# A gated cross-attention block with routed experts: the last four of 39 routed tiles in a block entered only when the count of used tiles is above 35

## The chip, the core and the metric

The kernel runs on one core of a Trainium2 chip. The metric is the time on the device in microseconds (us). Runs of the same program are summed up by their median. Beside them stands one profiled execution, from which every duration of a single instruction comes.

The engines are TensorE (PE in the profile; PEld is its weight load, PEldq its sequencer), VectorE (DVE), ScalarE (ACT), GpSimd (POOL) and SyncE (SP, which here only starts DMA transfers). Each has an instruction stream of its own, and they wait for each other by semaphores.

## What is computed

The reference is a cross-attention layer and a mixture-of-experts layer, both with a gate, on x of 4 x 512 rows of 256 numbers, all in 32-bit floats. Cut to what matters here:

```python
x = x + tanh(g_xattn[0]) * xattn(layernorm(x), ctx)   # 16 heads, 1601 context rows
h = layernorm(x)                                      # 2048 rows of 256
probs = sigmoid(h @ Wr.T + rb)                        # 8 routed experts
scores, idx = top_k(probs, 2)                         # 2 experts for each row
out = expert(h, shared)
for e in range(8):
    out = out + cw[..., e:e+1] * expert(h, e)         # cw: the score where e was picked, else 0
x = x + tanh(g_ffn[0]) * out
# expert(h, e) = (silu(h @ Wg.T) * (h @ Wu.T)) @ Wd.T, inner width 512
```

Each row has two picked experts, so there are 4096 pairs of row and expert. How they fall on the eight experts depends on the data.

## The kernel before, in words

The first three quarters of the time are the attention, with a written-out order of bursts; the change does not touch it. Then come the experts.

*Routing (find_places, invert, addresses).* The kernel computes only the picked pairs. It sorts the pairs by expert into tiles of 128 rows, and an expert's last tile may be partly empty. DVE counts the pairs per expert, derives how many tiles each expert uses (`used`, line 868) and sums these up along the experts (`end`, line 871), so that the last element of `end` is the number of used tiles. `tile_e` (line 912) holds the expert of each tile. Two small matrices, `token` and `dest`, hold for each tile the 128 source rows and the 128 result rows; where a tile has no pair, the address is out of bounds and the transfer of that row is dropped.

*The tiles.* The program is fixed before the data are known, so it has a tile for the worst case: `TILES = (TOP * NT + NR * (P - 1)) // P` is (2 * 2048 + 8 * 127) // 128 = 39 (line 110). The loop at line 1051 is unrolled over these 39. For tile i it has

- `own(i)` (line 1033): PE loads the tile's expert from `tile_e` into a register, which then selects the weights in `w_all`, where all eight experts lie;
- `half(i, gp, 0)` and `half(i, up, 2)` (line 993): the gate and the up product into PSUM, ahead of the second of them `turn(i - 1)`;
- the silu on ACT (line 1060) and the product `hid2[i]` on DVE (line 1062);
- `take(i + 1)` (line 984): PE turns the next tile's gathered rows, ACT copies them out of PSUM;
- `fetch(i + 3)` (line 973): POOL starts the gather of rows three tiles ahead, from `rows_x` into one of four buffers;
- `give(i - 1)` (line 1010): the down product of the tile before, a copy by DVE (line 1021), and the scatter by POOL into `rows_y` in HBM (line 1022). The scatters are declared free of each other.

`turn(i)` (line 1003) transposes `hid2[i]` on PE in four pieces, and ACT copies the result.

*Shared expert (fill).* The shared expert of all rows is cut into pieces; `fill(n)` places the next n of them where it stands. After the row of tiles two pieces stand, then `turn` of the last tile, one piece, and its `give`; then comes `fill(2 * NI)`, eight pieces (line 1100).

*The end.* Eight DMAs (line 1080) load `rows_y` into parts of `w_all` whose weights are used up; they wait for all scatters. `combine` (line 1085) adds the two weighted results to each row on DVE (line 1090) and starts the output DMAs (line 1095), among them four more pieces of the shared expert.

*Order.* From line 1037 on, a manual schedule keeps PE and POOL in the order of the text; the streams of ACT, DVE and SP are ordered by the framework's scheduler inside that part.

Of the kernel before, what the change touches and what calls it, by code (L numbers as in the profile page):

```python
# [8 lines left out]
FP = mybir.dt.float32  # L9
AF = mybir.ActivationFunctionType  # L10
# [15 lines left out]
def kernel(  # L26
# [782 lines left out]
    picks = [moe.tile(shp, FP, name=f"pick{k}") for k in range(TOP)]  # L809
    cws = [moe.tile([P, NTT], FP, name=f"cw{k}") for k in range(TOP)]  # L810
    tile_e = moe.tile([1, TILES], I32, name="tile_e")
    place = moe.tile([P, NJ], FP, name="place")
    at_tile = moe.tile([P, NJ], FP, name="at_tile")
    at_row = moe.tile([P, NJ], FP, name="at_row")
# [24 lines left out]
    def find_places():  # L839

        flat = both.rearrange("p t e -> p (t e)")
        before = ps_ms.tile([P, S], FP, tag="ms", name="before")[:, : NTT * NR]
        nc.tensor.matmul(before, lhsT=triu, rhs=flat, start=True, stop=True)
        total = ps_av.tile([P, S], FP, tag="av", name="total")[:, : NTT * NR]
        nc.tensor.matmul(total, lhsT=ones, rhs=flat, start=True, stop=True)
        tot = moe.tile(shp, FP, name="tot")
        nc.vector.tensor_copy(tot.rearrange("p t e -> p (t e)"), total)
        acc = [moe.tile(shp, FP, name=f"acc{k}") for k in range(2)]
        src, d, k = tot, 1, 0
        while d < NTT:  # L850
            dst = acc[k]
            nc.vector.tensor_copy(dst[:, :d, :], src[:, :d, :])
            nc.vector.tensor_tensor(
                dst[:, d:, :], src[:, d:, :], src[:, : NTT - d, :], ALU.add
            )
            src, d, k = dst, 2 * d, 1 - k
        count = src[:, NTT - 1, :]
        wide = [P, NR, NTT]
        full = moe.tile(wide, FP, name="full")
        marks = moe.tile([P, NTT], FP, name="marks")  # L860
        nc.vector.tensor_scalar(marks, steps[:, :NTT], float(P), None, ALU.mult)
        nc.vector.tensor_tensor(
            full,
            count.unsqueeze(2).to_broadcast(wide),
            marks.unsqueeze(1).to_broadcast(wide),
            ALU.is_gt,
        )
        used = moe.tile([P, NR], FP, name="used")
        nc.vector.tensor_reduce(used, full, AX.X, ALU.add)
        ends = [moe.tile([P, NR], FP, name=f"ends{k}") for k in range(2)]  # L870
        end, d, k = used, 1, 0
        while d < NR:
            dst = ends[k]
            nc.vector.tensor_copy(dst[:, :d], end[:, :d])
            nc.vector.tensor_tensor(dst[:, d:], end[:, d:], end[:, : NR - d], ALU.add)
            end, d, k = dst, 2 * d, 1 - k
        base = moe.tile([P, NR], FP, name="base")
        nc.vector.tensor_tensor(base, end, used, ALU.subtract)
        nc.vector.tensor_scalar(base, base, float(P), None, ALU.mult)
        row = moe.tile(shp, FP, name="row")  # L880
        nc.vector.tensor_tensor(row, src, tot, ALU.subtract)
        nc.vector.tensor_tensor(
            row, row, before.rearrange("p (t e) -> p t e", e=NR), ALU.add
        )
        nc.vector.tensor_tensor(
            row, row, base.unsqueeze(1).to_broadcast(shp), ALU.add
        )
        for k in range(TOP):
            nc.vector.tensor_tensor(hits, picks[k], row, ALU.mult)
            nc.vector.tensor_reduce(  # L890
                place[:, k * NTT : (k + 1) * NTT], hits, AX.X, ALU.add
            )

        nc.vector.tensor_scalar(
            at_tile, place, 1.0 / P, -(P - 1) / (2.0 * P), ALU.mult, ALU.add
        )
        nc.vector.tensor_scalar(at_tile, at_tile, 1.5 * 2.0**23, None, ALU.add)
        nc.vector.tensor_scalar(at_tile, at_tile, -1.5 * 2.0**23, None, ALU.add)
        nc.vector.scalar_tensor_tensor(
            at_row, at_tile, -float(P), place, ALU.mult, ALU.add  # L900
        )
        owner = [1, TILES, NR]
        past = moe.tile(owner, FP, name="past")
        nc.vector.tensor_tensor(
            past,
            end[0:1].unsqueeze(1).to_broadcast(owner),
            steps[0:1, :TILES].unsqueeze(2).to_broadcast(owner),
            ALU.is_le,
        )
        te = moe.tile([1, TILES], FP, name="te")  # L910
        nc.vector.tensor_reduce(te, past, AX.X, ALU.add)
        nc.vector.tensor_scalar(tile_e, te, float(NR - 1), None, ALU.min)


    PART = 8
# [68 lines left out]
    def take(i):  # L984
        ps = ps_ms.tile([P, S], FP, tag="ms", name="tx")[:, :H].rearrange(
            "p (c n) -> p c n", n=P
        )
        for c in range(2):
            nc.tensor.transpose(ps[:, c, :], xg[i % 4][:, c * P : (c + 1) * P], ident)  # L989
        xT[i] = work.tile([P, 2, P], FP, tag="xT", name=f"xT_{i}")  # L990
        nc.scalar.copy(xT[i], ps)  # L991

    def half(i, ps, off):
        for c in range(2):
            nc.tensor.matmul(  # L995
                ps,
                lhsT=xT[i][:, c, :],
                rhs=w_flat[:, bass.ds(owners[i] + (off + c) * I, I)],
                start=(c == 0),
                stop=(c == 1),  # L1000
            )

    def turn(i):
        ps = ps_av.tile([P, S], FP, tag="av", name="th").rearrange("p (f n) -> p f n", n=P)
        for f in range(NI):
            nc.tensor.transpose(ps[:, f, :], hid2[i][:, f * P : (f + 1) * P], ident)  # L1006
        hT2[i] = work.tile([P, NI, P], FP, tag="hT2", name=f"hT2_{i}")
        nc.scalar.copy(hT2[i], ps)
# [24 lines left out]
    def own(i):  # L1033
        e = nc.tensor.value_load(tile_e[0:1, i : i + 1], min_val=0, max_val=NR - 1)
        owners[i] = nc.tensor.snap(e * (6 * I))

    with tc.manual_schedule(engines={mybir.EngineType.PE, mybir.EngineType.Pool}):
        choose()
        fill(5)
        find_places()  # L1040
        fill(6)
        for part in range(NJ // PART):
            invert(part)
            fill(1)
        addresses()
        for i in range(3):
            fetch(i)
        weights()
        fill(3)
        take(0)  # L1050
        for i in range(TILES):
            own(i)
            gp = ps_g.tile([P, I], FP, tag="g", name="gp")
            half(i, gp, 0)
            if i:
                turn(i - 1)
            up = ps_u.tile([P, I], FP, tag="u", name="up")
            half(i, up, 2)
            sg = work.tile([P, I], FP, tag="sg")
            nc.scalar.activation(sg, gp, AF.Silu)  # L1060
            hid2[i] = work.tile([P, I], FP, tag="hid2", name=f"hid2_{i}")
            nc.vector.tensor_tensor(hid2[i], sg, up, ALU.mult)  # L1062
            if i + 1 < TILES:
                take(i + 1)
            fetch(i + 3)
            if i:
                give(i - 1)
        fill(2)
        turn(TILES - 1)
        fill(1)  # L1070
        give(TILES - 1)

        yk = {}
        for b in range(B):
            for k in range(TOP):
                yk[b, k] = w_all[:, TOP * b + k, 0:2, :].rearrange(
                    "p c (k h) -> p (c k) h", h=H
                )
                r = k * NT + b * S
                nc.sync.dma_start(  # L1080
                    out=yk[b, k],
                    in_=rows_y[r : r + S, :].rearrange("(t p) h -> p t h", p=P),
                )

        def combine(b):
            for t in range(NTB):
                for k in range(TOP):
                    xt = xs[b][:, t, :]
                    cw = cws[k][:, b * NTB + t : b * NTB + t + 1]
                    nc.vector.scalar_tensor_tensor(  # L1090
                        xt, yk[b, k][:, t, :], cw, xt, ALU.mult, ALU.add
                    )
                if t % 2:
                    r = b * S + (t - 1) * P
                    nc.sync.dma_start(
                        out=out[r : r + 2 * P, :].rearrange("(t p) h -> p t h", p=P),
                        in_=xs[b][:, t - 1 : t + 1, :],
                    )

        fill(2 * NI)  # L1100
        for b in range(2):
            combine(b)
        fill(NTB)
        for b in range(2, B):
            combine(b)
# [76 lines left out]
```

## Time and profile before

| | us |
|---|---|
| median of 3 runs | 1268.55 |
| lowest and highest | 1266.56 and 1268.7 |
| the profiled execution | 1266.34 |
| its span, first to last instruction | 1264.5 |
| first gate product of the tiles (PE, line 995) | 1004.64 |
| last gate product of the tiles starts | 1224.44 |
| last scatter (POOL, line 1022) | 1238.29 |
| first reload of results (SP, line 1080) | 1240.40 |

The span is the time between the first and the last instruction of one execution; the time of a run has about two microseconds more around it. In lines of a group, `x39` is the number of instructions, and a name like L1022 is the line of the source. In a line of the timeline the first number is the start, the second the duration of the group, and the bracket the time that the engine idled before it with what ended this. In windows each engine has its busy time and, in brackets, the number of its instructions. `<-` separates what is written from what is read.

### The profile page before, as it was taken

What the parts mean: (1) busy time and instruction counts of PE and PEld (TensorE: products, weight loads), DVE (VectorE), ACT (ScalarE), POOL (GpSimd) and SP (SyncE); (2) the same over time, 40 slices, a digit from 0 to 9 for tenths busy, and PEclk for the clock granted to TensorE, in tenths of its full rate; (3) what the DMA queues carried; (4) which work ended last, traced back from release to release, by engine and by line L of the source; (5) the groups of instructions that cost most, each with busy time, mean ns of one, the idle gap of its engine ahead of it and who ended that gap; (6) DMA issues with size and microseconds to landing.
All of it is one profiled execution on the core that took longest, in us unless ns stands there. A gap on an engine that the chain in (4) does not pass through costs nothing.

```text
span 1264.5 us, 19650 instructions
## 1 busy us (share of the span) xinstructions
PE 1246.0 (99%) x7742; PEld 558.7 (44%) x7742; DVE 686.9 (54%) x1294; ACT 592.6 (47%) x1139; POOL 133.7 (11%) x213
## 2 busy tenths in 40 slices
PE   7999999999999999999999999999999999999998
PEld 3533334333343433344343333344256566666665
DVE  5977666666676665666656656676026411121125
ACT  2265555556545555564565556555822122222220
POOL 2000200000013000000400000020000133333320
PEclk9999999999999999999999999999999999999999
DMA  5312000002001000200010000000092011111106
GB/s 123 102 40 64 1 14 14 1 1 53 14 1 31 14 2 1 53 14 1 4 27 14 1 13 14 1 18 1 1 335 81 18 38 42 47 40 43 35 9 199
DMA packets 30992, 48.29 MB, mean 38 GB/s; under 512 B 5487, under 2 KB 21745, under 8 KB 30902
## 3 DMA queue, kind: packets, MB, share of 16 engines
q1 hardware_dynamic: 26628, 38.14, 11.5%
q0 software_dynamic: 3744, 8.40, 2.1%
q8 instruction: 62, 1.02, 0.3%
q10 hardware_dynamic: 530, 0.50, 0.2%
q14 instruction: 28, 0.23, 0.1%
HBM read 32.99 MB, written 9.31 MB: 33 GB/s over the span
## 4 chain that ended last, share of the span: by engine, by line
PE 95%; DVE 2%; DMA 1%; issue 1%; ACT 0%; SPq 0%; DVEq 0%; ACTq 0%
PE sc L420 32%; PE av L441 17%; PE gp L995 5%; PE y_ps L1013 5%; PE up L995 5%; PE mx L361 4%; PE ms L338 4%; PE ms L312 3%; PE ms L490 3%; PE ms L293 3%; PE ms L502 2%; PE up L720 2%; PE gp L720 1%; PE th L1006 1%; PE sc L361 1%; PE op L743 1%
## 5 line engine op out<-in xcount | busy, mean ns | idle before, releaser
L372 DVE TENSOR_REDUCE mxs<-mx 128x1 f32<-128x512 f32 x744 | 480.1, 686 | 251.0 <-PE mx L361 247.1
L429 ACT ACTIVATE es<-sc 128x512 f32<-128x512 f32 x804 | 437.6, 594 | 341.1 <-PE mx L361 291.5
L361 PE MATMUL mx<-ks,qT 32*128 32x512 f32 (+1 forms) x1984 | 480.7, 549 | 0.0
L420 PE MATMUL sc<-qA,ks 32*128 32x512 f32 x1608 | 467.6, 637 | 0.8 <-DVE qA L415 0.8
L420 PEld LDWEIGHTS sc<-qA,ks 32*128 32x128 f32 x1608 | 131.2, 179 | 221.8 <-issue 165.3
L441 PE MATMUL av<-es,vs 128*32 128x512 f32 (+2 forms) x1864 | 227.8, 559 | 0.1
L361 PEld LDWEIGHTS mx<-ks,qT 32*128 32x128 f32 x1984 | 164.7, 183 | 4.0 <-issue 1.9
L441 PEld LDWEIGHTS av<-es,vs 128*32 128x32 f32 (+1 forms) x1864 | 37.1, 108 | 166.1 <-issue 161.2
L1062 DVE TENSOR_TENSOR hid<-sg,up 128x512 f32<-128x512 f32 x39 | 26.8, 688 | 138.2 <-PE up L995 138.2
L243 POOL TENSOR_SCALAR var<-var 128x4 f32<-128x4 f32 x6 | 1.4, 237 | 782.9 <-DVE first L240 782.9
L1060 ACT ACTIVATE sg<-gp 128x512 f32<-128x512 f32 x39 | 23.3, 597 | 115.7 <-PE gp L995 115.7
L995 PE MATMUL gp<-w_all,xT 128*128 x156 | 73.5, 593 | 0.9 <-ACT xT L991 0.9
L1013 PE MATMUL y_ps<-w_all,hT 128*128 x312 | 73.8, 379 | 0.0
L995 PE MATMUL up<-w_all,xT 128*128 x156 | 73.4, 593 | 0.0
L1013 PEld LDWEIGHTS y_ps<-w_all,hT 128*128 128x128 f32 x312 | 56.4, 190 | 6.5 <-issue 0.5
L338 PE MATMUL ms<-wv_t,ctx_t 96*128 96x256 f32 (+1 forms) x208 | 58.7, 404 | 0.1
L1022 POOL DMA_INDIRECT rows_y<-y,dest x39 | 39.5, 1014 | 149.1 <-DVE y L1021 149.1
L338 PEld LDWEIGHTS ms<-wv_t,ctx_t 96*128 96x128 f32 (+1 forms) x208 | 34.5, 185 | 37.9 <-issue 27.3
L975 POOL DMA_INDIRECT xg<-rows_x,token x39 | 40.2, 1030 | 48.1 <-DVE token L959 36.5
L312 PE MATMUL ms<-ctx_t,wk_t 96*128 96x401 f32 (+3 forms) x112 | 45.1, 524 | 0.0
L1021 DVE COPY y<-y_ps 128x256 f32<-128x256 f32 x39 | 16.6, 425 | 46.2 <-PE y_ps L1013 46.2
L991 ACT COPY xT<-tx 128x256 f32<-128x256 f32 x39 | 14.6, 375 | 54.5 <-PE tx L989 54.5
(164 smaller groups left out, 963.5 us busy)
## 6 DMA issues: line engine op xcount, KB each, us to landing
ks<-kd SPq DMA_DIRECT2D x63, 100.1 KB, 3.2
w_all<-in_wgT SPq DMA_DIRECT2D x8, 512.0 KB, 11.0
w_all<-in_wuT SPq DMA_DIRECT2D x8, 512.0 KB, 10.1
w_all<-in_wdT SPq DMA_DIRECT2D x8, 512.0 KB, 11.0
w_all<-rows_y SPq DMA_DIRECT2D x8, 512.0 KB, 8.3
ctx_t<-in_ctxT SPq DMA_DIRECT2D x3, 1200.8 KB, 8.0
xb<-in_x SPq DMA_DIRECT2D x4, 512.0 KB, 6.2
rows_x<-xn SPq DMA_DIRECT2D x4, 512.0 KB, 3.3
```

Source lines behind the costliest of these rows:

```text
L312: nc.tensor.matmul(ps[:, :n], lhsT=wk_t[r, c, h2 * P : (h2 + 1) * P], rhs=ctx_t[r, c, o : o + n], start=(c == 0), stop=(c == 1),)
L338: nc.tensor.matmul(ps[:n, : NH * HD], lhsT=ctx_t[r, c, o : o + n], rhs=heads[r, c, :, :HD], start=(c == 0), stop=(c == 1),)
L361: nc.tensor.matmul(ps[:, n * REST : (n + 1) * REST] if last else ps, lhsT=qT[i][slot_of(j), qb * P : (qb + 1) * P], rhs=ks[i % 3][slot_of( ...
L372: nc.vector.tensor_reduce(mxs[i][:, qb, j, c : c + 1], ps, AX.X, ALU.max)
L420: nc.tensor.matmul(ps[:n, :], lhsT=ks[i % 3][r, o : o + n], rhs=qA[i][r, :], start=True, stop=True)
L429: nc.scalar.activation(es[(i * NKT + kt) % 2, j][:n], ps[:n], AF.Exp, scale=SCALE)
L441: nc.tensor.matmul(av[i][j * HS : (j + 1) * HS, cols], lhsT=v_of(b, kt)[:n, g * HPG + j, :], rhs=es[(i * NKT + kt) % 2, j][:n, cols], star ...
L720: nc.tensor.matmul(ps, lhsT=w_sh[:, off + c, f * P : (f + 1) * P], rhs=x2T[:, c, b * S : (b + 1) * S], start=(c == 0), stop=(c == 1),)
L975: nc.gpsimd.indirect_dma_start(out=xg[i % 4], out_offset=None, in_=rows_x, in_offset=bass.IndirectOffsetOnAxis(ap=token[:, i : i + 1], axi ...
L995: nc.tensor.matmul(ps, lhsT=xT[i][:, c, :], rhs=w_flat[:, bass.ds(owners[i] + (off + c) * I, I)], start=(c == 0), stop=(c == 1),)
L1013: nc.tensor.matmul(ps, lhsT=hT2[i][:, f, :], rhs=w_flat[:, bass.ds(owners[i] + 4 * I + f * H, H)], start=(f == 0), stop=(f == NI - 1),)
L1022: ins = nc.gpsimd.indirect_dma_start(out=rows_y, out_offset=bass.IndirectOffsetOnAxis(ap=dest[:, i : i + 1], axis=0), in_=y, in_offset=Non ...
```

## The change

The body of the loop becomes a function `run_tiles(first, end)`. It is called for tiles 0 to 34 where the loop stood; `SURE` is 4096 // 128 + 8 // 2 - 1 = 35. Tiles 35 to 38 are called again inside `tc.If(n_used[0] > SURE)`, with a `take` of tile 35 ahead of them and `turn` and `give` of tile 38 behind. The two fills, the `turn` and the `give` that followed tile 38 now follow tile 34, ahead of the block. The count is copied to an integer, `tiles_used`, in `find_places`, and each of the five engines loads it into a register at tile 33. What follows the row of tiles stands in a manual schedule of its own behind the block. `fetch(i + 3)` still runs for tiles 35 to 37 ahead of the block.

The diff:

```diff
--- before.py
+++ after.py
@@ -809,6 +809,7 @@
     picks = [moe.tile(shp, FP, name=f"pick{k}") for k in range(TOP)]
     cws = [moe.tile([P, NTT], FP, name=f"cw{k}") for k in range(TOP)]
     tile_e = moe.tile([1, TILES], I32, name="tile_e")
+    tiles_used = moe.tile([1, 1], I32, name="tiles_used")
     place = moe.tile([P, NJ], FP, name="place")
     at_tile = moe.tile([P, NJ], FP, name="at_tile")
     at_row = moe.tile([P, NJ], FP, name="at_row")
@@ -910,6 +911,7 @@
         te = moe.tile([1, TILES], FP, name="te")
         nc.vector.tensor_reduce(te, past, AX.X, ALU.add)
         nc.vector.tensor_scalar(tile_e, te, float(NR - 1), None, ALU.min)
+        nc.vector.tensor_copy(tiles_used, end[0:1, NR - 1 : NR])
 
 
     PART = 8
@@ -1033,6 +1035,30 @@
     def own(i):
         e = nc.tensor.value_load(tile_e[0:1, i : i + 1], min_val=0, max_val=NR - 1)
         owners[i] = nc.tensor.snap(e * (6 * I))
+
+    def run_tiles(first, end):
+        for i in range(first, end):
+            own(i)
+            gp = ps_g.tile([P, I], FP, tag="g", name="gp")
+            half(i, gp, 0)
+            if i > first:
+                turn(i - 1)
+            up = ps_u.tile([P, I], FP, tag="u", name="up")
+            half(i, up, 2)
+            sg = work.tile([P, I], FP, tag="sg")
+            nc.scalar.activation(sg, gp, AF.Silu)
+            hid2[i] = work.tile([P, I], FP, tag="hid2", name=f"hid2_{i}")
+            nc.vector.tensor_tensor(hid2[i], sg, up, ALU.mult)
+            if i + 1 < end:
+                take(i + 1)
+            fetch(i + 3)
+            if i > first:
+                give(i - 1)
+            if i == SURE - 2:
+                n_used.append(nc.values_load(tiles_used, min_val=0, max_val=TILES))
+
+    n_used = []
+    SURE = TOP * NT // P + NR // 2 - 1
 
     with tc.manual_schedule(engines={mybir.EngineType.PE, mybir.EngineType.Pool}):
         choose()
@@ -1048,27 +1074,18 @@
         weights()
         fill(3)
         take(0)
-        for i in range(TILES):
-            own(i)
-            gp = ps_g.tile([P, I], FP, tag="g", name="gp")
-            half(i, gp, 0)
-            if i:
-                turn(i - 1)
-            up = ps_u.tile([P, I], FP, tag="u", name="up")
-            half(i, up, 2)
-            sg = work.tile([P, I], FP, tag="sg")
-            nc.scalar.activation(sg, gp, AF.Silu)
-            hid2[i] = work.tile([P, I], FP, tag="hid2", name=f"hid2_{i}")
-            nc.vector.tensor_tensor(hid2[i], sg, up, ALU.mult)
-            if i + 1 < TILES:
-                take(i + 1)
-            fetch(i + 3)
-            if i:
-                give(i - 1)
+        run_tiles(0, SURE)
         fill(2)
-        turn(TILES - 1)
+        turn(SURE - 1)
         fill(1)
-        give(TILES - 1)
+        give(SURE - 1)
+    with tc.If(n_used[0] > SURE):
+        with tc.manual_schedule(engines={mybir.EngineType.PE, mybir.EngineType.Pool}):
+            take(SURE)
+            run_tiles(SURE, TILES)
+            turn(TILES - 1)
+            give(TILES - 1)
+    with tc.manual_schedule(engines={mybir.EngineType.PE, mybir.EngineType.Pool}):
 
         yk = {}
         for b in range(B):
```

## The prediction

> **What bounds the kernel now.** I read the page first: busy shares, the clock row and the chain that ended last.
>
> ```profile
> PE 1246.0 (99%) x7742; PEld 558.7 (44%) x7742; DVE 686.9 (54%) x1294; ACT 592.6 (47%) x1139; POOL 133.7 (11%) x213
> ...
> PEclk9999999999999999999999999999999999999999
> ...
> PE 95%; DVE 2%; DMA 1%; issue 1%; ACT 0%; SPq 0%; DVEq 0%; ACTq 0%
> ```
>
> TensorE (PE) is busy for 99% of the span, in no slice below nine tenths of its clock, and carries 95% of the chain. PE work that goes away is worth its whole duration, as long as nothing takes its place. The second view is the busy time in windows: two of the last tiles, cut at the starts of their gate products (gp of tiles 36, 37 and 38), and the tail from just before the last result ends.
>
> ```profile
> core 0: us, PE busy (x) PEld busy (x) DVE busy (x) ACT busy (x) POOL busy (x), PEclk, DMA share, GB/s
> 1212.80:1218.62 5.82, 5.82 (x23) 3.60 (x22) 1.11 (x2) 1.45 (x3) 1.02 (x1) 1.00 0.05 19
> 1218.62:1224.44 5.82, 5.82 (x23) 3.60 (x22) 1.11 (x2) 1.45 (x3) 1.00 (x1) 1.00 0.01 0
> 1237.39:1264.50 27.11, 21.07 (x65) 11.89 (x63) 17.60 (x41) 2.39 (x4) 0.98 (x1) 1.00 0.70 232
> ```
>
> A tile takes 5.82 us, all of it PE at full clock; DVE needs 1.11 us of that and ACT 1.45. In the last 27 us DVE (17.60 us) and the DMA (0.70) come up beside PE: there a shorter PE alone would not move the end.
>
> Third, the DMA view of 1219 to 1239.5 us, in which the results of tiles 35 to 38 are scattered:
>
> ```profile
> q0 software_dynamic: 144, 0.00, 0.5%
> ...
> rows_y<-y,dest POOLq DMA_INDIRECT x4, 2.1
> ```
>
> Four scatters move 0.00 MB. The scatter of tile 34 (POOL, at 1213.71 us) lies in the first window above: 19 GB/s over 5.82 us are 110 KB, about 105 rows of 1 KB; the next window has none. So tile 34 holds rows and tiles 35 to 38 hold none: the count that the chip will read is 35, and 35 > 35 is false. The reference's routing, worked through for these inputs, agrees: 523, 614, 883, 116, 674, 638, 543 and 105 pairs per expert fill 5+5+7+1+6+5+5+1 = 35 tiles of 128.
>
> Fourth, the timeline from the last result to the end:
>
> ```profile
> 1235.66 1.89 PE L1013 MATMUL y_ps<-w_all,hT 128*128 x8
> ...
> 1238.29 0.98 POOL L1022 DMA_INDIRECT rows_y<-y,dest  x1 [6.36 <-DVE y L1021]
> ...
> 1240.40 7.83 SPq L1080 DMA_DIRECT2D w_all<-rows_y  x8
> ...
> 1244.40 0.88 DVE L1090 SCALAR_TENSOR_TENSOR xb<-w_all,cw,xb 128x256 f32<-128x256 f32 x2 [2.62 <-DMA w_all<-rows_y]
> ...
> 1249.41 1.88 PE L720 MATMUL up<-x2T,w_sh 128*128 128x512 f32 x4
> ...
> 1252.87 0.69 DVE L738 TENSOR_TENSOR hT<-sg,up 128x512 f32<-128x512 f32 x1
> ```
>
> Two strands run to the end: last result, copy, scatter, reload by DMA, combine on DVE; and beside it eight pieces of the shared expert on PE. They meet on DVE, which hardly rests from 1244.40 to 1261.4. PE has some room: its last up ends at 1251.29 and DVE takes it up at 1252.87, 1.6 us later; at the second of four pieces the room is 0.8, with 0.45 us of DVE idling behind it, 1.2 in all. I use 1.4.
>
> **The change, part by part.** Removed is the PE work of four tiles. The order around them stays: the fills and the last turn and give surround tile 34 as they did tile 38. So four whole steady periods go, 4 x 5.82 = 23.28 us. Of 39 gathers one is skipped (fetch 38), of 39 scatters four; they are empty and lie beside PE, worth 0.
>
> The last scatter has rows now. Tile 38's landed 2.1 us after its issue, empty; tile 34's moves 105 KB. The nearest row is that of the gathers, which landed in 2.2 (an empty one) to 2.9 us (a full one). I take +0.3 us (0 to 0.8) on the reload strand. One more DVE copy of one element stands in find_places; the nearest row is tile_e's on line 912, 164 ns. PE works on fills there; 0 to 0.2, I take 0.1.
>
> Five register loads of tiles_used come at tile 33, one per engine. The load of tile_e on PE has the price, with register arithmetic of 151 ns in the row after it:
>
> ```profile
> L1034 PEldq TENSOR_LOAD <-tile_e x39: 296/301/496, 1003.2 to 1222.1; - x39
> ```
>
> Some 0.45 us each. The last begins at 1222.1 us, and the gp that it serves at 1224.44: PE's sequencer runs 2.3 us ahead of its array, so tile 33's two loads, 0.9 us, stay under that cover (without it they would cost 0.5). What they wait for was written at about 979 us. Behind DVE's load stand hid and the y copy, behind ACT's the silu, behind POOL's the scatter; by the timeline these three idle 3.5, 3.0 and 3.5 us in each tile, and SP only waits there. I take 0.
>
> The block itself can only be bounded, since no branch stands in the trace. Below: each engine compares its own register and jumps, PE's jump under the 2.3 us lead. That is 0, and not less, because no tail can start before its data. Above: every engine must have finished and the last scatter landed before any goes on. From the end of the last y_ps (1237.55) copy, scatter and landing take until 1240.40, 2.85 us; 0.3 for the rows; 0.4 for a meeting of the engines (the program's end, after the last output has landed, has two in under 1 us). PE idles 3.5 us; less its room of 1.4, 2.1 us on the path, and SP's 0.7 us lie within that. Between: engines finish their own instructions, but no DMA is waited for. PE then waits until POOL's scatter is issued (1239.27), 1.7 us, +0.3 to meet, less 1.4 of room: 0.6. I take this 0.6. An engine's semaphore count must come out the same whether or not the block ran, so something has to be settled at the jump, but the landing has a wait of its own at line 1080.
>
> Two rules of the Trainium skill speak against the change. "Runtime: NRT & Kernel Launch", Instruction fetch mechanics: instructions stream in sequential blocks, and a jump to a target outside the two at hand waits for a fetch. The page has 62 packets, 1.02 MB, on an instruction queue: 16.5 KB each, one per 250 of PE's 15,484 matmuls and weight loads. The block holds 4 x 44 = 176 of these, with register instructions some 210, under one packet; on the other engines under 20. By the row the target is at hand and costs 0; if the rule bites, my estimate is one to two small landings in a row, 2 to 4 us. I go by the row. "TensorE: Matmul & The Clock Gate", Part 1: after an idle window of about 3.4 us PE runs at half clock for about as long. The clock row shows no such case, PE not idling so long in this phase; at 2.0 us idle it adds nothing, but the upper bound's 3.5 us sit on the threshold, and half speed for 3.4 us costs 1.7.
>
> The sum, the two strands added because DVE takes up both: -23.28 + 0.3 + 0.1 + 0.6 = -22.3 us. The profiled execution took 1266.34 us (span 1264.5 and 1.8 around it): it would take 1244.0. The median of the runs shown, 1268.55, is 2.2 above it; from there, 1246.2. I state the latter; the range takes in the former.
>
> **The rivals.** First, the engines meet at the block with the DMA included, and the reload strand's wait becomes everybody's. For it: all engines must agree, and the scatters count on semaphores of their own. Against it: no data makes PE wait. 2.1 + 0.1, with slow clock 3.9, in place of 1.0: 1247.4 to 1249.1.
>
> Second, PE's jump waits for instructions: 2 to 4 us on top of its 2.0, with no room left to hide them, 1248.2 to 1250.2. For it is the rule, against it the packet's size. The others' jumps would hide in their idle time.
>
> Third, slower: the block is entered. It decides at 36 used tiles; the expert with 638 pairs would need three more. Then no tile is saved and the row of tiles is cut in two. Tile 35's transposes and ACT copy come before its gp with no give to cover them (0.6 us); at the block's end turn waits for hid (PE's up ends 1228.48, hid 1229.28: 0.8) and give for the copy of th (0.8): together 2.2, and at the block's start and end 0.6 to 3.8 each. +3.4 to +9.8: 1272 to 1278. The empty scatters speak against it.
>
> That the block is skipped and the time not given back would need DVE or DMA to bind in the tile phase; they are busy 1.11 of 5.82 us and 5%.
>
> **How the numbers follow.** The likeliest case has 0.62 (own range 1243.5 to 1247.5), the first rival 0.24, the second 0.08, the third 0.03; 0.03 is for another order of DVE and ACT in a part now scheduled by itself, which may eat any share of the gain. This measurement tells about 0.2%, 2.5 us, from no change. Faster 0.95, same 0.02, slower 0.03. The range runs from the full 23.3 us below the quickest run (1266.56), 1243, to the second rival's end and a little slow clock, 1251.
>
> **What would show it.** Right: 35 scatters, and 156 - 16 = 140 gp matmuls of the tiles; a last scatter 22 to 24 us earlier; a PE gap of about 2 us between the last y_ps and the next gp of the shared expert; from the last scatter to the end 26 to 28 us (26.2 before). Wrong: that gap above 3 us, ending when the scatter lands (first rival), a clock under 1 behind it, a jump after which PE waits for nothing shown (second), 39 scatters (third). Tiles of other than 5.82 us would mean that the cut has disturbed the row itself.

## The result and the profile after

The changed kernel takes 1248.03 us in the median of 4 runs (1247.88 to 1248.13). Beside them 4 runs of the kernel before had a median of 1267.61 (1266.56 to 1268.7). The ratio is 0.9845, with an interval of 0.9828 to 0.9862. The profiled executions took 1266.34 us before and 1248.13 after: 18.2 us less, where the prediction's sum had 22.3. The forecast of 1246.2 was 1.8 us low, and the time lies in the range, but outside the likeliest case's own range (1243.5 to 1247.5).

The counts and windows of the page came as predicted. First the busy shares, the clock and the chain that ended last, from the page of the changed kernel:

```profile
PE 1224.7 (98%) x7654; PEld 545.2 (44%) x7654; DVE 683.4 (55%) x1287; ACT 586.7 (47%) x1127; POOL 128.7 (10%) x208
...
PEclk9999999999999999999999999999999999999999
...
PE 1%; DMA 1%; DVE 0%; SPq 0%; issue 0%; DVEq 0%
...
L997 PE MATMUL gp<-w_all,xT 128*128 x140 | 66.0, 593 | 0.9 <-ACT xT L993 0.9
```

PE's busy time falls by 21.3 us and the gate products go from 156 to 140: four tiles are gone. The chain that ended last was followed back for only 2 or 3% of the span, to PE's first product behind the block; the profile has no releaser there and stops. It therefore tells about the tail alone, and that PE's 95% are missing from it is no finding.

The windows, one tile (from the gp of tile 33 to that of tile 34) and the tail from just before the last scatter, and the DMA view of 1193 to 1217 us:

```profile
1195.81:1201.63 5.82, 5.82 (x24) 3.60 (x22) 1.11 (x2) 1.45 (x3) 2.04 (x2) 1.00 0.08 25
1215.40:1246.30 30.90, 22.55 (x64) 12.68 (x62) 18.00 (x40) 2.39 (x4) 1.00 (x1) 0.91 0.63 207
```

```profile
q0 software_dynamic: 288, 0.30, 3.9%
...
rows_y<-y,dest POOLq DMA_INDIRECT x4, 2.4
```

A tile still takes 5.82 us, all PE. The packets of three scatters fall into the DMA view; those of the last one, of tile 34, are in the view of 1213 to 1219 us, and carry rows too:

```profile
q0 software_dynamic: 48, 0.11, 5.2%
```

The new thing is in the second window: the tail is longer, and PE's clock in it is 0.91, where it was 1.00.

The timeline from the last result to the end (PE, DVE, POOL and SP; some rows left out):

```profile
1212.85 1.89 PE L1015 MATMUL y_ps<-w_all,hT 128*128 x8
...
1215.04 1.95 PE L720 MATMUL gp<-x2T,w_sh 128*128 128x512 f32 x4 [0.30 <-PEq L1082]
1215.48 1.00 POOL L1024 DMA_INDIRECT rows_y<-y,dest  x1 [6.33 <-DVE y L1023]
1216.83 1.88 PE L720 MATMUL up<-x2T,w_sh 128*128 128x512 f32 x4
...
1217.97 7.93 SPq L1097 DMA_DIRECT2D w_all<-rows_y  x8
...
1221.97 0.48 DVE L1107 SCALAR_TENSOR_TENSOR xb<-w_all,cw,xb 128x256 f32<-128x256 f32 x1 [6.77 <-DMA w_all<-rows_y]
...
1222.37 0.68 DVE L738 TENSOR_TENSOR hT<-sg,up 128x512 f32<-128x512 f32 x1
...
1230.77 2.85 DVE L1107 SCALAR_TENSOR_TENSOR xb<-w_all,cw,xb 128x256 f32<-128x256 f32 x7
...
1233.54 0.68 DVE L738 TENSOR_TENSOR hT<-sg,up 128x512 f32<-128x512 f32 x1
...
1234.28 7.38 PE L743 MATMUL op<-w_sh,hT 128*128 128x256 f32 x26 [2.67 <-DVE hT L738]
```

And two lines of the kernel before that answer to the hT and op lines:

```profile
1241.10 0.69 DVE L738 TENSOR_TENSOR hT<-sg,up 128x512 f32<-128x512 f32 x1 [3.08 <-PE up L720]
...
1253.61 5.88 PE L743 MATMUL op<-w_sh,hT 128*128 128x256 f32 x26 [1.03 <-DVE hT L738]
```

Read it from the top. At the jump PE stands still for 0.30 us. The last scatter starts at 1215.48, 22.81 us earlier than before (1238.29). The reload follows 2.49 us later (2.11 before). Then DVE takes up a combine *first* and idles 6.77 us until the first reload has landed. The first hT (silu of the gate times up, a product of the shared expert that its down product `op` on PE needs) stands behind it at 1222.37, though its up product was done at 1218.71. Before, DVE made that hT at 1241.10, ahead of the first combine. Counted from the last scatter, the four hT start at 2.81, 6.90, 11.21 and 14.58 us before, and at 6.89, 10.75, 14.69 and 18.06 us after. The last is 3.48 us later. The whole timelines show what stands ahead of it on DVE: 23 combines after, 17 before. Seven combines take 2.85 us, 0.41 each, so my estimate for the six more is 2.5 us; 0.6 is the first hT, which DVE used to make while it waited for the reload; 0.38 is the later start of the reload. Together that is 3.5 us. From the last hT to the last instruction it is 11.62 us before and 12.74 after, 1.12 more. The gain in the profiles is therefore -22.81 + 3.48 + 1.12 = -18.2 us.

The 1.12 have to do with the 26 down products, which take 7.38 us in place of 5.88. The windows of the changed kernel show the clock behind it (after PE's busy time come PEld, DVE, ACT and POOL, then the granted clock, DMA share and GB/s):

```profile
1225.00:1230.00 5.00, 4.87 (x14) 2.24 (x12) 4.92 (x13) 0.60 (x1) 0.00 (x0) 1.00 1.05 343
1230.00:1235.00 5.00, 1.42 (x4) 0.94 (x5) 4.62 (x11) 0.00 (x0) 0.00 (x0) 0.89 1.09 367
1235.00:1240.00 5.00, 5.00 (x20) 4.19 (x19) 2.94 (x7) 0.00 (x0) 0.00 (x0) 0.77 0.26 92
```

Between 1230 and 1235 us PE waits for hT twice, 1.03 and 2.67 us, and in the next window it is busy throughout at a clock of 0.77. The windows of before are all at 1.00.

One thing has to be known for the comparisons below: executions of every kernel here, the one before too, differ by some 2.2 us ahead of the experts (in five of the twelve profiles PE runs at half clock for 3.4 us there, and their first gate product starts at 1007.2 to 1007.9 us, in the other seven at 1004.6 to 1005.5), so I compare tails (last scatter to last instruction) in the traces, and ratios of runs on one chip.

### The profile page after: what moved, and what is told of

It is laid out like the page before. It is cut to its first block, busy times and chain, and to the rows that moved or that the text cites. A ratio compares the mean times of both kernels' runs of the same rounds, so it can differ in the third digit from the quotient of the medians.

```text
span 1246.3 us, 19395 instructions
## 1 busy us (share of the span) xinstructions
PE 1224.7 (98%) x7654; PEld 545.2 (44%) x7654; DVE 683.4 (55%) x1287; ACT 586.7 (47%) x1127; POOL 128.7 (10%) x208
## 5 line engine op out<-in xcount | busy, mean ns | idle before, releaser
L1051 DVE TENSOR_TENSOR hid<-sg,up 128x512 f32<-128x512 f32 x35 | 24.1, 688 | 124.2 <-PE up L997 124.2
L1049 ACT ACTIVATE sg<-gp 128x512 f32<-128x512 f32 x35 | 20.9, 597 | 103.8 <-PE gp L997 103.8
L997 PE MATMUL gp<-w_all,xT 128*128 x140 | 66.0, 593 | 0.9 <-ACT xT L993 0.9
L1015 PE MATMUL y_ps<-w_all,hT 128*128 x280 | 66.2, 379 | 0.0
L997 PE MATMUL up<-w_all,xT 128*128 x140 | 65.9, 593 | 0.0
L1015 PEld LDWEIGHTS y_ps<-w_all,hT 128*128 128x128 f32 x280 | 50.6, 190 | 5.9 <-issue 0.5
L1024 POOL DMA_INDIRECT rows_y<-y,dest x35 | 35.6, 1016 | 131.1 <-DVE y L1023 131.1
L736 ACT ACTIVATE sg<-gp 128x512 f32<-128x512 f32 x16 | 9.6, 597 | 62.7 <-PE gp L720 49.7
L374 DVE TENSOR_REDUCE mxs<-mx 128x4 f32<-128x260 f32 x62 | 23.8, 425 | 26.4 <-PE sc L420 22.5
```

What stands on the lines that cost most here:

```text
L997: nc.tensor.matmul(ps, lhsT=xT[i][:, c, :], rhs=w_flat[:, bass.ds(owners[i] + (off + c) * I, I)], start=(c == 0), stop=(c == 1),)
L1015: nc.tensor.matmul(ps, lhsT=hT2[i][:, f, :], rhs=w_flat[:, bass.ds(owners[i] + 4 * I + f * H, H)], start=(f == 0), stop=(f == NI - 1),)
L1024: ins = nc.gpsimd.indirect_dma_start(out=rows_y, out_offset=bass.IndirectOffsetOnAxis(ap=dest[:, i : i + 1], axis=0), in_=y, in_offset=Non ...
```

## The experiments

My theory: the change's own parts (cut, loads, jump) cost about what was forecast, and the missing 4 us come from the order of DVE behind the block, which the scheduler chose anew because that part is now scheduled by itself: DVE waits for a reload with hT queued behind it. The expectations call this the order theory. Rivals: the jump or the meeting of the engines holds up the reload (the settling theory of the expectations); or the full last scatter and the cut disturb the tail.

**The order by hand.** In the changed kernel DVE joins the manual schedule behind the block, and its combines and fills are written in about the order that the kernel before had. The block stays.

```diff
-    with tc.manual_schedule(engines={mybir.EngineType.PE, mybir.EngineType.Pool}):
+    with tc.manual_schedule(
+        engines={mybir.EngineType.PE, mybir.EngineType.Pool, mybir.EngineType.DVE}
+    ):
...
-        fill(2 * NI)
-        for b in range(2):
-            combine(b)
...
+        for word in "F2 00 00 F2 00 01 01 01 00 10 01 10 F2 11 11 10 10 11 11 20 F2 21 20 20 F1 21 21 20 F1 21 30 30 F1 31 31 30 31 F1 30 31".split():
+            if word[0] == "F":
+                fill(int(word[1]))
+            else:
+                add(int(word[0]), int(word[1]))
```

> The changed kernel with the block, but DVE's order behind the block written out by hand as it stood before the change: the first product of the shared expert (line 738) ahead of the first combine, and the three others in their old places. Order theory (the scheduler gave DVE another order behind the block; the first product then waits for the reload, PE waits for DVE 2.7 us longer and then runs at a lower clock for some 1.5 us): 4.2 us less than the changed kernel, 1243.3 to 1244.5 us, no clock below 1. Settling theory (what the block itself waits for, the semaphores at the jump and the later reload, costs the missing 4 us): unchanged, 1247.5 to 1248.5 us.

Measured: 1245.07 us (1244.14 to 1245.63), ratio 0.9820 (0.9805 to 0.9835), 0.6 us above the order theory's figures. Its timeline, the first hT and the 26 down products:

```profile
1219.03 0.69 DVE L738 TENSOR_TENSOR hT<-sg,up 128x512 f32<-128x512 f32 x1 [3.62 <-PE up L720]
...
1225.66 2.86 DVE L1111 SCALAR_TENSOR_TENSOR xb<-w_all,cw,xb 128x256 f32<-128x256 f32 x7 [1.62 <-issue]
...
1232.53 5.88 PE L743 MATMUL op<-w_sh,hT 128*128 128x256 f32 x26 [2.02 <-DVE hT L738]
```

hT now starts 3.34 us after the last scatter, not 6.89, the last hT stands behind 17 combines again, the down products take 5.88 us, and the tail is 27.74 us instead of 30.80. That is most of what was missing. What is left, 1.5 us over the tail of before, stands in the middle line: DVE still idles 1.62 us there, ahead of combines of later rows; the profile names no releaser (issue), and by its place it is a later reload.

**The old program with 35 tiles.** No block, no loads, no count: only the row is cut. The four tiles left out hold no rows.

```diff
-        for i in range(TILES):
+        SURE = TOP * NT // P + NR // 2 - 1
+        for i in range(SURE):
...
-            if i + 1 < TILES:
+            if i + 1 < SURE:
...
-        turn(TILES - 1)
+        turn(SURE - 1)
```

> The kernel before with 35 tiles in place of 39 and nothing else: no block, no copy of the count, no register loads; the four tiles left out hold no rows for these inputs. Both theories: the four tiles are worth 23.28 us and the last scatter's rows cost 0.2 to 0.4, so 23 us less than before, 1244.0 to 1245.0 us. The theories part in the distance to e1_order. Order theory: the block, copy and loads together cost 0.3 to 0.8 us, so e1_order lies that much above this one. Settling theory: e1_order lies 3 to 4 us above.

Measured: 1245.10 us (1242.99 to 1246.64), ratio 0.9819 (0.9802 to 0.9836), and a tail of 26.58 us. hT starts 2.80 us after the last scatter, as before. So the cut and the full last scatter add 0.4 us to the tail of 26.19. The runs can't tell this kernel from the one with the block and the order by hand (0.9820): by the medians no cost of the block itself shows, but they would not show one of 1 or 2 us either.

**The new order in the old program.** All 39 tiles, no block; only DVE joins a manual schedule in the last part, and its order there is written out as the changed kernel has it.

```diff
+    with tc.manual_schedule(
+        engines={mybir.EngineType.PE, mybir.EngineType.Pool, mybir.EngineType.DVE}
+    ):
...
+        for word in "00 F2 00 00 01 01 01 00 10 F2 01 11 10 10 11 11 10 20 F2 11 21 20 20 21 21 20 F2 21 F1 30 31 F1 30 31 F1 30 31 F1 30 31".split():
```

> The kernel before, all 39 tiles and no block, with its tail given the order that DVE has in the changed kernel (one combine ahead of the first product). Order theory: 3.5 to 4.5 us more than before, 1271 to 1272.5 us, with PE waiting for DVE ahead of the last down products and a clock below 1 behind it. Settling theory: no difference, 1267 to 1268.5 us.

Measured: 1273.14 us (1270.91 to 1274.15), ratio 1.0042 (1.0027 to 1.0057). The tail is 29.93 us, 3.74 more than before. Its timeline has the signs of the changed kernel, in a program without any branch:

```profile
1247.04 0.48 DVE L1095 SCALAR_TENSOR_TENSOR xb<-w_all,cw,xb 128x256 f32<-128x256 f32 x1 [6.41 <-DMA w_all<-rows_y]
1247.44 0.68 DVE L738 TENSOR_TENSOR hT<-sg,up 128x512 f32<-128x512 f32 x1
...
1255.30 0.70 PE L743 MATMUL op<-w_sh,hT 128*128 128x256 f32 x2 [0.54 <-DVE hT L738]
...
1258.67 7.57 PE L743 MATMUL op<-w_sh,hT 128*128 128x256 f32 x26 [2.67 <-DVE hT L738]
```

DVE waits for the reload ahead of hT, 23 combines stand ahead of the last hT, PE waits the same 2.67 us, and the 26 down products take 7.57 us. The order alone makes the loss. In the medians it is larger than in the profile and than was expected: 1273.14 against 1266.17, of which the 2.2 us of the earlier part may be a share.

**PE kept busy.** The changed kernel, with four matmuls of 512 columns into a spare PSUM tile where PE waits for the third and fourth hT. Nothing reads them.

```diff
+    def busy(n):
+        ps = ps_ms.tile([P, S], FP, tag="ms", name="busy")
+        for k in range(n):
+            nc.tensor.matmul(ps, lhsT=ident, rhs=w_sh[:, 0, :], start=True, stop=True)
...
+                if b == B - 1 and t == 0 and f >= 2:
+                    busy(2 * f - 3)
```

> The changed kernel, with four extra matmuls of 512 columns on PE whose results nobody reads, placed where PE waits for DVE in the first of the last four down products (1 ahead of the third part, 3 ahead of the fourth). Clock theory (the wait lowers the granted clock, which lengthens the down products by about 1.5 us): 1.0 to 1.6 us less than the changed kernel, 1246.4 to 1247.0 us, clock row at 1. If the low clock comes from something else, or DVE sets the end anyway: unchanged or up to 0.5 us more, 1248.0 to 1248.5 us.

Measured: 1249.56 us (1247.55 to 1250.22), ratio 0.9852 (0.9836 to 0.9869); the expectation missed. The part at which it was aimed did what was said:

```profile
1233.65 0.70 PE L750 MATMUL op<-w_sh,hT 128*128 128x256 f32 x2 [0.23 <-DVE hT L743]
1234.18 2.74 PE L717 MATMUL busy<-w_sh,ident 128*128 128x512 f32 x6
...
1237.01 5.88 PE L750 MATMUL op<-w_sh,hT 128*128 128x256 f32 x26
```

With PE busy the clock is 1.00 in the windows from 1230 to 1245 us, the 26 products take 5.88 us, and from the start of the last hT to the end it is 11.25 us against 12.74. So the slow products are the clock's doing. But in this profile the third hT stands 15.35 us behind the last scatter, against 14.69: a later reload (DVE idles 0.63 us for it at 1228.58) took 0.7 of the 1.5 us back, and the tail is 29.97. The median shows no gain because it is mixed with the earlier part: the profiled execution and two others lie some 2 us above the remaining two (1247.55 and 1247.80), which are 0.1 to 0.6 us quicker than the four of the changed kernel, on another chip.

**The block taken out of the changed kernel.** The copy of the count, the five register loads and the part of its own remain; the `If` and the tiles in it, which hold no rows, go.

```diff
-    with tc.If(n_used[0] > SURE):
-        with tc.manual_schedule(engines={mybir.EngineType.PE, mybir.EngineType.Pool}):
-            take(SURE)
-            run_tiles(SURE, TILES)
-            turn(TILES - 1)
-            give(TILES - 1)
```

> The changed kernel without the block and its four tiles (which hold no rows for these inputs), but with everything else of the change: the copy of the count, the five register loads, and the two manual schedules with a cut between them. It has the order of DVE that the kernel before has, so the cut alone does not move it. Order theory: tail of 26.4 to 27 us, as the 35-tile kernel without any of it (26.6), so copy, loads and cut cost at most 0.4 us in all. Settling theory: the loads and the cut cost something that can be seen, a tail of 28 us or more.

Measured: 1244.09 us (1243.40 to 1244.62), ratio 0.9811 (0.9795 to 0.9828), tail 26.04 us. Its timeline:

```profile
1218.67 0.69 DVE L738 TENSOR_TENSOR hT<-sg,up 128x512 f32<-128x512 f32 x1 [3.08 <-PE up L720]
...
1231.02 5.88 PE L743 MATMUL op<-w_sh,hT 128*128 128x256 f32 x26 [0.86 <-DVE hT L738]
```

hT is back in its place, 2.80 us after the last scatter, although the last part stands in a manual schedule of its own here too. So it is the conditional block ahead of it, not the second schedule, that made the scheduler order what follows anew. Copy and loads cost nothing that the tail shows.

**The block entered.** `SURE` is 34, so the count of 35 is above it, and all 39 tiles are computed.

```diff
-    SURE = TOP * NT // P + NR // 2 - 1
+    SURE = TOP * NT // P + NR // 2 - 2
```

> The changed kernel with its threshold and its cut one tile lower: 34 tiles ahead of the block, and tiles 34 to 38 in the block, which is entered since 35 > 34. All 39 tiles are computed. The prediction's third rival priced this at 3.4 to 9.8 us more than before. With what the runs since have shown (the jump costs PE 0.3 us; behind the block DVE's order costs 3 to 4 us), order theory: 0.9 at the block's start, 1.6 at its end, 0.5 for settling, 4 for the order: 6 to 8 us more than before, 1273 to 1275 us against 1266 to 1268. Settling theory: the engines meet at both ends with the DMA included, 10 us or more above before.

Measured: 1277.19 us (1275.18 to 1278.00), ratio 1.0074 (1.0057 to 1.0091), 8.7 us above the kernel before on the same chip, where 6 to 8 was expected. The profile divides it: the last scatter starts at 1241.63, 3.34 us later than before (0.8 of this lies ahead of the first tile), and the tail is 31.72 us, 5.53 longer. At the end of the block the give waits for ACT:

```profile
1238.89 1.99 PE L1015 MATMUL y_ps<-w_all,hT 128*128 x8 [0.73 <-ACT hT L1010]
```

So the price of a count above the bound is mostly the same tail, and only some 2.5 us the cut row of tiles.

**Two pieces ahead of the block.** A repair without an order by hand: one fill more stands ahead of the block, so that its hT can't be put behind a combine.

```diff
         give(SURE - 1)
+        fill(2)
     with tc.If(n_used[0] > SURE):
...
-        fill(2 * NI)
+        fill(2 * NI - 2)
```

> The changed kernel with one thing moved: the first two of the eight shared pieces stand ahead of the block, behind the give of tile 34, so that their product on DVE (line 738) cannot be ordered behind the first combine; the scheduler orders the rest by itself. Order theory: as with the order by hand, the tail (last scatter to the end) falls from 30.8 to 27 to 28 us, no clock below 1 in the down products, 3 to 4 us less than the changed kernel on the same chip. Settling theory: the block's own waits stay and the tail stays at 30 us or more.

Measured: 1244.97 us (1243.89 to 1245.36), ratio 0.9819 (0.9806 to 0.9832), tail 27.62 us.

```profile
1218.70 0.69 DVE L738 TENSOR_TENSOR hT<-sg,up 128x512 f32<-128x512 f32 x1 [3.08 <-PEq L1083]
...
1232.39 5.88 PE L743 MATMUL op<-w_sh,hT 128*128 128x256 f32 x26 [1.66 <-DVE hT L738]
```

The first hT is back at 2.80 us. The scheduler still puts one combine ahead of the second hT, but its reload lands at 1222.67, about when the second up product ends (1222.56), so the second hT loses only half a microsecond. The last hT stands behind 16 combines. No run here takes the wait of the first hT without the six more combines ahead of the last, or the reverse.

**The same kernels again.** The changed kernel ran twice more, on the chips of the experiments, and the one with the order by hand once.

> The changed kernel unaltered, on the same chip as the runs beside it, to have its tail (from the start of the last scatter to the end of the span) a second time. Expected 30 to 31 us of tail as in its first profile (30.8), and a median within 1 us of 1248 us.

> The changed kernel unaltered, for the comparison on one chip with the two runs beside it: tail of 30.8 to 31.1 us, 3 to 4 us above them by the order theory, level with them by the settling theory.

> The changed kernel with DVE's order by hand a second time, now beside the unaltered changed kernel on one chip. Order theory: 3 to 4 us less than the changed kernel. Its first profile had a tail of 27.7 us, of which 1.6 us was DVE waiting for the second reload; if that wait comes with the block it will be there again, otherwise the tail is near 26.5 us.

Measured for the changed kernel: 1250.43 us (1248.57 to 1252.76), ratio 0.9867 (0.9848 to 0.9886), tail 31.03, its median 2.4 us above 1248 where 1 was allowed for; then 1252.28 (1249.66 to 1253.06), ratio 0.9876 (0.9859 to 0.9893), tail 32.32. For the order by hand: 1244.52 (1243.90 to 1247.41), ratio 0.9821 (0.9807 to 0.9834), tail 27.25. These last two and the kernel with pieces ahead ran on one chip; there the changed kernel is 7.3 to 7.8 us behind both, twice what was expected. Why its third set is the slowest, its timeline shows:

```profile
1233.78 0.70 PE L743 MATMUL op<-w_sh,hT 128*128 128x256 f32 x2 [1.00 <-DVE hT L738]
...
1237.15 8.40 PE L743 MATMUL op<-w_sh,hT 128*128 128x256 f32 x26 [2.67 <-DVE hT L738]
```

The waits are those of the first profile, but the 26 products took 8.40 us instead of 7.38 and, between 1237.4 and 1242.4 us, a clock of 0.51. The rest of its distance, 2.4 us, lies ahead of the last scatter (1217.87 against 1215.48), and is the early half clock. Its median lies above the prediction's range.

## Why the prediction was right or wrong

**Block skipped, four periods gone: right.** There are 35 scatters and 140 gate products, and a tile stays at 5.82 us. The last scatter moved by 22.81 us against a forecast of 23.28 less 0.1. Of the difference 0.24 is the DVE copy with what surrounds it, at the routing, and 0.23 lies ahead of it and is not of the change.

**The last scatter with rows, +0.3: right.** The reload starts 2.49 us behind it in place of 2.11, +0.38; 2.41 in the old program with 35 tiles.

**Loads at tile 33, 0: right.** They took 305 ns on PE and 472 to 546 ns on the others, and the kernel without the block, which keeps them, has the shortest tail (26.04 us).

**The block, 0.6: its size is not refuted, its working is.** I had PE wait for POOL's scatter, 2.0 us. It waited 0.30 and went on before the scatter was issued; its branch ran under the sequencer's lead:

```profile
L1082 PEldq EVENT_SEMAPHORE  x2: 51/51/51, 1214.8 to 1214.9; - x2
...
L1082 ACTq COMPARE_BRANCH  x1: 54/54/54, 1211.9 to 1211.9; - x1
...
L1082 PEldq COMPARE_BRANCH  x1: 369/369/369, 1212.4 to 1212.4; - x1
...
L1082 POOLq INC_SWDGE_SEM  x1: 1651/1651/1651, 1215.6 to 1215.6; - x1
```

These are the instructions of the block's line: each engine's branch took 45 to 72 ns, PE's 369, 2.6 us ahead of the gp that it stood before. The 0.30 lie at PE's two semaphore instructions, which ran when its last product had ended (1214.74). POOL spends 1.65 us on one of its own, up to 1217.3, some 0.6 us before the scatter had landed (2.4 us after its start); no engine's wait is put down to it. With the old order restored, the three profiles with the block have tails of 27.25, 27.62 and 27.74 us, the two without it 26.58 and 26.04. The means differ by 1.2 us; the medians (ratios of 0.9819 to 0.9821 against 0.9819 and 0.9811) can't tell them apart. What there is of it shows as DVE waiting for the later reloads: SP's group of eight takes 8.62 to 8.86 us in these three and 7.34 to 7.95 in these two. Why, I have not found.

**The failed step: the tail behind the block, "26 to 28 us".** It was 30.8, and 31.0 and 32.3 in the repeats. I carried the tail over with the old order on DVE, gave another order no time in the sum and kept 0.03 for "another order of DVE and ACT in a part now scheduled by itself". That case came. It costs 3.74 us where it was tried alone in the old program. In the changed kernel the mean of the three tails (31.4) is 3.8 above the three with the order restored (27.5). It consists of hT behind a combine that waits for a DMA, of 23 combines in place of 17 ahead of the last hT, and of a clock that falls when PE then waits for hT: 7.28 to 8.40 us for the 26 products in place of 5.88.

**The clock rule: too mild here.** The prediction weighed the Trainium skill, "TensorE: Matmul & The Clock Gate", Part 1, at 3.4 us of idling; PE's longest wait in the tail is 2.67. The same page says that the clock is set by windows of this length which run freely. The changed kernel's trace agrees when it is cut where the clock changes:

```profile
1230.52:1233.93 3.41, 0.70 (x2) 0.30 (x2) 3.41 (x9) 0.00 (x0) 0.00 (x0) 1.00 1.09 366
1233.93:1237.34 3.41, 3.06 (x7) 2.52 (x8) 2.14 (x5) 0.00 (x0) 0.00 (x0) 0.50 0.73 255
1237.34:1240.75 3.41, 3.41 (x17) 2.97 (x16) 2.20 (x5) 0.00 (x0) 0.00 (x0) 1.00 0.01 5
```

The first window holds most of the longer wait, the end of the shorter one and 0.70 us of matmuls, and the whole next one is at half clock. PE was busy for 3.06 us of it, so 1.5 us are lost: the 7.38 in place of 5.88. In the five profiles with the new order and no filler PE was busy for 0.70 to 1.66 us of the window ahead of the fall, so it need not be idle throughout. The half clock then lasts for one window, or for two (8.40 us, and 8.25 with the block entered), and that is why equal waits cost different times. With the order by hand a window with a wait of 1.52 us and 1.89 us of work kept the clock. Where the limit lies is open: early in the kernel the clock fell in four profiles after a window with 2.63 us of work, and in one after a full one.

**The rivals.** First, the meeting with the DMA included (1247.4 to 1249.1): the time fell into its range, but PE's wait of 0.30 us refutes it. A clock under 1 came, one of its signs, but behind PE's waits for hT. Second, the jump that waits for instructions: a fetch is there. In the DMA view of 1212 to 1216 us the changed kernel has the line below, and the same kernel without the block has none of it.

```profile
q8 instruction: 1, 0.02, 2.0%
```

It is one block of 16 KB, 1.2 us behind PE's branch and 1.25 us long, and comes 12 us after the one before it; in the kernel before that distance was 28 us. PE's array had work for that time. In the kernel with two pieces ahead of the block PE's branch ran 6.0 us ahead of its array (1212.9), and the gap at the jump is the same, so it is not the fetch's:

```profile
1218.89 1.95 PE L720 MATMUL gp<-x2T,w_sh 128*128 128x512 f32 x4 [0.30 <-PEq L1083]
```

Whether this is the fetch of the rule ("Runtime: NRT & Kernel Launch", Instruction fetch mechanics) or the next block in sequence, called earlier by the jump, the trace does not say: the page of the profile has 62 packets on that queue before and after. The row I went by was right about the price. Third, the block entered, +3.4 to +9.8: measured +8.7, but with the order's share in it, which that rival did not have.

Had the scheduler kept its order, the change would have brought 1244.5 to 1245.1 us, 21 to 23 us less than the kernel before on the same chips (1266.17 and 1267.92); the forecast was 22.3. That the measured time lies in the range, and only 1.8 us from the forecast, is luck. In the profiles 4.1 us of the gain are missing: an order came that I had given no time of its own. But the forecast started from 1268.55 us, an execution that by its time has the 2.2 us of the earlier part, and the four of the changed kernel by theirs have not.

## What to carry to other kernels

A conditional block was a border for the scheduler here: ask not only what the engines do at the jump, but in which order each engine that is not ordered by hand will be put behind it, whether its first instruction now waits for a DMA with ready work queued behind it, and how much comes ahead of the product that the longest engine waits for. Independent work moved ahead of the block (two pieces here) or an order by hand got 3.8 us of tail back, 3 to 7 us by the ratios (0.9845 to 0.9876 against 0.982), which have the early half clock in them. PE reached the branch with work still in its array, and its array stood for 0.30 us, the instruction fetch included; the tails with the block are 1.2 us longer than those without, for a reason that was not found.

## What the runs showed of the hardware

- In the tail PE's clock was halved for 3.41 us or for 6.83 us at a time, after windows of 3.41 us in which PE had worked 0.70 to 1.66 us (waits of 0.54 to 1.08 and 2.67 us); it stayed with 1.89 us of work and a wait of 1.52 us. In five profiles it was halved for 3.41 us long before, in one of them with no wait of PE in the trace.
- PE's compare-and-branch took 369 ns, those of the other four engines 45 to 72 ns.
- Behind the taken jump on PE a block of 16 KB was fetched; the gap in PE's array was 0.30 us, whether the branch ran 2.6 or 6.0 us ahead of it.
- A load of one register from on-chip memory took 305 ns on PE and 472 to 546 ns elsewhere.
